# Order of layernorm parts and a third head on ScalarE in a fused two-layer transformer kernel

## The chip, the cores and the metric

The kernel runs on one core of a Trainium2 chip. A core has TensorE for matrix products, VectorE, ScalarE and GpSimd for elementwise work, and a SyncE that issues DMAs. Each works through its own queue, and they meet at semaphores. In the profile they are PE (PEld for its weight loads), DVE, ACT, POOL and SP. The metric is the device time of one execution in microseconds (us).

## The reference: what is computed

Two layers, each an attention and a feed-forward block, wrapped as `x = x + layernorm(block(layernorm(x)))`. The change lies in the second attention. It runs on 4 sequences (rows) of 1024 tokens with 256 features, in 16 heads of 16:

```python
scores = jnp.einsum('bhqd,bhkd->bhqk', q, k) / jnp.sqrt(jnp.asarray(HD, q.dtype))
w = jax.nn.relu(scores)
return w / (jnp.sum(w, axis=-1, keepdims=True) + KERN_EPS)
...
out = jnp.einsum('bhqk,bhkd->bhqd', attn, v)
out = out.transpose(0, 2, 1, 3).reshape(Bx, Sx, D)
out = out @ w_out + b_out
y = x + out
mu = jnp.mean(y, axis=-1, keepdims=True)
var = jnp.var(y, axis=-1, keepdims=True)
return (y - mu) * jax.lax.rsqrt(var + LN_EPS) * gamma + beta
```

The weights are a relu of the scores, divided by their sum; there is no exponential. The result is normalized once more and added to `x`, and the layernorm of that sum goes to the mixture-of-experts block that follows.

## The kernel before

**Stages.** The first layer ends at about 420 us, the second attention runs to about 1005 us, and the experts fill the rest. Only the second attention is touched.

**Tiling of the attention.** Loops run over rows (`b`, 4), blocks of 512 queries (`qh`, 2 per row), groups of four heads (`g`, 4) and tiles of 128 keys (`kt`, 8). The very last block is cut in two halves of 256 queries (`q2`, `halves = 2`), and a step then takes two key tiles. That makes 64 steps per row. One step is:

- `scores` (line 1489): 8 matmuls (16 in the last block), line 1501, for four heads. Two heads go to single PSUM banks (tag `s`, three buffers, also used by every other small product in the stage) and two to the halves of one two-bank tile `pair` (tag `d`, two buffers).
- The relu into `w`: ScalarE takes the two single heads (line 1510), VectorE the pair in one instruction over 1024 columns (line 1515). With `all_on_act` ScalarE takes the pair too (line 1513).
- `weigh` (line 1522), for scores of two steps earlier: the value matmuls of line 1527, which add into the one accumulator `po`. After the last key tile of a group, `finish` has VectorE transpose `po` into `turned` (line 1583), and the next group's first value matmuls must wait for that.

**Pieces and parts.** Everything else in the stage is cut into `Part` objects and worked in between. Those in `beside` are *pieces*, with matmuls of their own: transposes, keys, queries and values of the next row (`project`), the output projection (`project_out`, line 1292, evacuated by VectorE at line 1298), the transposes for the gate (`turn_gating`, line 1342) and the gate's logits (`gate`). Those in `rest` are called parts here: layernorm steps by tile of 128 tokens (statistics on VectorE, lines 1125 to 1127; the power on GpSimd, line 1128; centring, line 1303; `shift` on ScalarE, line 1315; the sum into `x` on VectorE, line 1320; the rows for the experts with their DMA stores, `token_rows`), the division by the weights' sum (`divide`, lines 1257 to 1267) and the fetching of keys.

**The planner.** The Python that writes the instructions keeps `late`, the work owed by VectorE, ScalarE and GpSimd in us. A step subtracts what the engine has to spare in it, a piece adds what it costs there and subtracts its time on TensorE, and a part is issued while the debt stays within `MOST` (0.8, 0.2, 0.4). A part can need others to have been called, some steps (`age`) before. In this stage the order on TensorE, VectorE and ScalarE is the order in which the Python issues.

**One step in the order of issue.** `scores` with its relus; then `go_on_with_oldest`, which calls `finish` and the piece (the piece first where `fresh` says that the last group's end had none); then `go_on`, which issues the parts that fit. So a part stands behind the piece's evacuation in the queues of VectorE and ScalarE.

**Which steps put all heads on ScalarE.** Steps with a piece of more than 1.5 us on TensorE; in the last row also one step per group.

Of the kernel before, what the change touches and what calls it, by code (L numbers as in the profile page):

```python
# [14 lines left out]
ALU = mybir.AluOpType  # L15
# [59 lines left out]
def kernel(  # L75
# [32 lines left out]
    nc = tc.nc  # L108
# [113 lines left out]
    with ExitStack() as st1:  # L222
# [96 lines left out]
        for r in range(2):  # L319
            for j in range(4):  # L320
                at = 32 * j + HD * r
# [29 lines left out]
        def open_row(hs=None, last=False):  # L351

            row = {"h": hs or [act4("h") for _ in range(BPB)], "last": last}
            row["q"], row["kT"] = {}, {}
            row["q_d"] = [[dram.tile([2 * P, 2, TB], F32, name="q_d") for _ in range(DC)] for _ in range(BPB)]
            row["k_d"] = [[dram.tile([2 * P, TB], F32, name="k_d") for _ in range(DC)] for _ in range(BPB)]

            row["v"] = act_v("vaug")
            return row
# [14 lines left out]
        def fetch_queries(row, k, t):  # L374

            q = row["q"][k, t] = acts.tile([P, 2, 2, TB], F32R, tag="gate", name="q")
            nc.gpsimd.dma_start(
                q.rearrange("p r s n -> p r (s n)"), row["q_d"][k][t].rearrange("(r p) s n -> p r (s n)", p=P)
            )
# [138 lines left out]
        class Chain:  # L518
# [11 lines left out]
            def finish(self):  # L530
                while self.steps:
                    self.go()
# [468 lines left out]
        def woven(left, own, to_hidden):  # L1001

            return [
                *left[:2], *own[:2], *left[2:], *own[2:-2],
                *to_hidden[:1], *own[-2:-1], *to_hidden[1:2], *own[-1:], *to_hidden[2:],
            ]  # L1010

        left, ffn, take = [], ([], [], []), {}
        for t in range(NB):
# [38 lines left out]
            beside = woven(left, own, to_hidden)  # L1052
# [49 lines left out]
    with ExitStack() as st3:  # L1102
# [74 lines left out]
        def in_order(parts):  # L1177

            return [parts[at] for at in sorted(parts, key=lambda at: (2.5 * at[0] + at[1], at))]

        def normalize(row, b, k):

            h, x = row["h"][k], xs[b * BPB + k]

            def stats(i):
                return scale_of("a", x[:, i, :])

            def apply(i, rs, ms):
                scaled(h[:, i, :], x[:, i, :], rs, ms)

            return by_tile((stats, 0, STATS), (apply, 2, {"pool": 0.6}))
# [294 lines left out]

            return [start]

        def scores(row, qh, q2, halves, g, kt, all_on_act):

            t, r = divmod(g, 2)
            n = TB // halves
            q0 = q2 * n
            w = wts.tile([P, 4, TB], F32, tag="w", name="w")
            singles = [ps.tile([P, TB], F32, tag="s", name="sc1", bufs=3) for _ in range(2)]
            pair = ps.tile([P, 2, TB], F32, tag="d", name="sc2", bufs=2)
            for m in range(halves):
                for part in (1, 0):
                    for j, sc in enumerate((*singles, pair[:, 0, :], pair[:, 1, :])):
                        rows = slice(32 * j, 32 * (j + 1))  # L1500
                        nc.tensor.matmul(  # L1501
                            sc[:, m * n : (m + 1) * n],
                            lhsT=row["kT"][t][rows, r, (kt + m) * P : (kt + m + 1) * P],
                            rhs=row["q"][qh, t][rows, r, part, q0 : q0 + n],
                            start=(part == 1),
                            stop=(part == 0),
                        )

            for j, sc in enumerate(singles):
                nc.scalar.activation(w[:, j, :], sc, AF.Relu)  # L1510
            if all_on_act:

                nc.scalar.activation(w[:, 2:4, :], pair, AF.Relu)  # L1513
            else:
                nc.vector.tensor_scalar(w[:, 2:4, :], pair, 0.0, None, ALU.max)  # L1515
            return w

        def weighed(halves, r):
# [19 lines left out]
        beside, rest = [], []  # L1538

        late, MOST = [0.0, 0.0, 0.0], (0.8, 0.2, 0.4)  # L1540

        def take(part):

            for i, us in enumerate(part.takes):
                late[i] += us - part.tensor
            part()

        def next_piece(keep=0):

            could = [part for part in beside if part.ready()]  # L1550
            return could[0] if len(could) > keep else None

        def do_piece(part):

            if part is not None:
                beside.remove(part)
                take(part)

        def go_on():

            k = 0
            while k < len(rest):
                part = rest[k]
                if part.ready() and all(us == 0.0 or l + us <= m for us, l, m in zip(part.takes, late, MOST)):
                    del rest[k]
                    take(part)
                    k = 0
                else:
                    k += 1
# [24 lines left out]
        row = row0  # L1594
        for k in range(BPB):
            add_bias(row, k)
        waiting, fresh = [], [False]

        def go_on_with_oldest(piece):

            at = waiting.pop(0)
            if fresh[0]:
                do_piece(piece)
            finish(*at)
            if ends(at):
                late[0] += 0.65 / at[4]
            if not fresh[0]:
                do_piece(piece)
            fresh[0] = ends(at) and (fresh[0] or piece is None)

        def ends(at):

            return at[6] == KT - at[4]

        def piece_for(at):

            soon_ends = at[4] == 1 and 1 < KT - at[6] <= 3
            return next_piece(1 if soon_ends and not fresh[0] else 0)

        for b in range(B):  # L1620
            after = open_row(None if b else next_hs, last=b + 2 == B) if b + 1 < B else None
            for qh in range(BPB):
                if (b, qh) == (B - 1, BPB - 1):

                    nc.scalar.activation(spare, row["h"][qh][:, 0, 0:1], AF.Exp)
                if after is not None:
                    ahead = normalize(after, b + 1, qh)
                    rest.extend(in_order(ahead))
                    rest.append(
                        Part(  # L1630
                            lambda to=(after, qh): beside.extend(project(*to)),
                            [(x, 1) for x in ahead.values()],
                        )
                    )
                halves = 2 if (b, qh) == (B - 1, BPB - 1) else 1
                for q2 in range(halves):
                    for g in range(NG):
                        for kt in range(0, KT, halves):
                            Part.now += 1
                            piece = piece_for(waiting[0]) if len(waiting) > 1 else None  # L1640
                            on_act = piece is not None and piece.tensor > 1.5
                            on_act = on_act or row["last"] and kt // halves % (8 // halves) == 4 // halves
                            w = scores(row, qh, q2, halves, g, kt, on_act)
                            waiting.append((row, b, qh, q2, halves, g, kt, w))
                            step = kt // halves
                            if step == 1 and g % 2 == 0:
                                if g == 0 and q2 == 0:
                                    fetch_queries(row, qh, 1)
                                elif g and halves == 1:
                                    fetch_queries(*((row, 1) if qh == 0 else (after, 0)), 0)  # L1650
                            for i, us in enumerate((1.62, -0.5, 1.62) if on_act else (0.4, 0.53, 1.62)):
                                late[i] -= us
                            if len(waiting) > 2:
                                go_on_with_oldest(piece)
                            go_on()
                            late[:] = [max(x, 0.0) for x in late]
            row = after
        while waiting:
            finish(*waiting.pop(0))
        while beside or rest:  # L1660
            Part.now += 1
            assert Part.now < 2000
            late[:] = [-2.0, -2.0, -2.0]
            do_piece(next_piece())
            go_on()
        state["close"][0](*divide(state, DC - 1))
    both.close()
# [4 lines left out]
    with ExitStack() as st4:  # L1672
# [260 lines left out]
        last = lists[NE - 1]  # L1933
# [294 lines left out]
```

## Time and profile before

| | us |
|---|---|
| median of 3 runs | 1529.57 |
| lowest, highest | 1524.9, 1531.48 |
| the profiled execution | 1527.67 |
| its span on the core | 1525.9 |

| 420 to 988 us of that span | TensorE | VectorE | ScalarE | GpSimd |
|---|---|---|---|---|
| busy, us of 568 | 550.4 | 419.0 | 383.7 | 172.4 |

| line | what | count | mean, ns |
|---|---|---|---|
| 1510 | ScalarE relu of one head, 512 columns | 512 | 595 |
| 1513 | ScalarE relu of two heads, 1024 columns | 63 | 1033 |
| 1515 | VectorE relu of two heads, 1024 columns | 193 | 1219 |
| 1583 | VectorE transpose of a group's result | 36 | 649 |
| 1298 | VectorE evacuation of an output projection, 512 columns | 15 | 692 |
| 1315 | ScalarE shift of a layernorm | 30 | 510 |

A row of the trace's groups and timelines reads: start and duration in us, engine, line, operation, what is written from what, count; in brackets the idle time just before it and what ended it. Two relus of ScalarE that run back to back are shown as one row of about 1.08 us. Busy time is an average over the stage; what a change is worth is read from the places where TensorE stands still. The ends of matmuls are modelled, so distances are taken from start to start.

### The profile page before, as it was taken

The page shows a single profiled execution, that of the slowest core. Times are in us where ns is not written, and L with a number is a line of the kernel's source. Part 1 is how long each engine was busy: PE and PEld are TensorE (multiplying, and loading weights), DVE is VectorE, ACT ScalarE, POOL GpSimd, SP SyncE. Part 2 cuts the span into 40 slices and gives each one's busy share as a digit, 9 for nine tenths or more (in the row PEclk, how much of TensorE's full clock was granted, in tenths as well). Part 3 has the DMA queues.
Part 4 walks back from the last instruction along what each step waited for, and adds up shares of the span by engine and source line. Part 5 has one row for each costly group of instructions (what it writes and reads, how often), then busy time and mean ns, then how long its engine had stood idle before and what let it go on. Part 6 is the DMA issues. An engine that isn't in the chain of part 4 may idle for free. (4 is left out here: it accounts for less than half of the span.)

```text
span 1525.9 us, 24163 instructions
## 1 busy us (share of the span) xinstructions
PE 1462.9 (96%) x9286; PEld 787.0 (52%) x9286; DVE 887.4 (58%) x2128; ACT 685.0 (45%) x1160; POOL 495.7 (32%) x627
## 2 busy tenths in 40 slices
PE   8999999999899999999999999849999999999996
PEld 4666666667532323332333325427566656665674
DVE  5456654656457598759775887675545631212145
ACT  4244455443466666766666677622221122112142
POOL 4123232222341223422432223303425233242554
PEclk9999999999999999999999999979999999999998
DMA  8400000003423331542244211151314234233264
GB/s 217 131 1 1 1 1 1 1 0 117 120 83 125 94 108 49 166 120 87 64 147 138 70 50 36 43 156 38 100 28 116 49 73 94 53 78 77 65 162 128
DMA packets 91885, 121.58 MB, mean 80 GB/s; under 512 B 24925, under 2 KB 64250, under 8 KB 91642
## 3 DMA queue, kind: packets, MB, share of 16 engines
q1 hardware_dynamic: 70000, 73.09, 15.5%
q0 software_dynamic: 21712, 46.94, 13.3%
q8 instruction: 73, 1.20, 0.3%
q14 instruction: 42, 0.34, 0.1%
q10 hardware_dynamic: 58, 0.01, 0.0%
HBM read 66.90 MB, written 53.12 MB: 79 GB/s over the span
## 5 line engine op out<-in xcount | busy, mean ns | idle before, releaser
L1510 ACT ACTIVATE w<-sc 128x512 f32<-128x512 f32 x512 | 278.0, 595 | 141.9 <-ACT w L1510 60.4
L1527 PE MATMUL po<-w,vaug 128*17 128x512 f32 (+1 forms) x2304 | 270.1, 552 | 11.6 <-DVE turned L1583 11.3
L1515 DVE TENSOR_SCALAR w<-sc 128x1024 f32<-128x1024 f32 x193 | 234.4, 1219 | 43.2 <-PE sc L1501 37.1
L2110 ACT ACTIVATE hid<-ph,mb 128x512 f32<-128x512 f32 (+1 forms) x136 | 89.9, 662 | 340.5 <-PE ph L2103 244.7
L2103 PE MATMUL ph<-xT,w 128*128 128x512 f32 (+1 forms) x544 | 229.7, 574 | 0.3 <-DVE xT L2086 0.3
L2120 PE MATMUL py<-w,hid 128*128 128x256 f32 x1024 | 229.7, 380 | 0.0
L2120 PEld LDWEIGHTS py<-w,hid 128*128 128x128 f32 x1024 | 191.7, 190 | 31.7 <-issue 6.7
L1501 PE MATMUL sc<-q,kT 32*128 32x512 f32 (+1 forms) x2304 | 195.2, 413 | 6.9 <-DVE w L1515 4.8
L1501 PEld LDWEIGHTS sc<-q,kT 32*128 32x128 f32 x2304 | 88.4, 184 | 182.4 <-ACT w L1510 122.6
L2141 POOL DMA_INDIRECT acc_d<-y,idx x56 | 88.6, 1582 | 226.1 <-DVE y L2140 101.3
L2103 PEld LDWEIGHTS ph<-xT,w 128*128 128x128 f32 x544 | 99.7, 190 | 107.6 <-issue 98.4
L2139 DVE TENSOR_TENSOR y<-py,mb 128x256 f32<-128x256 f32 x56 | 23.5, 420 | 126.7 <-PE py L2120 116.0
L1527 PEld LDWEIGHTS po<-w,vaug 128*17 128x17 f32 x2304 | 41.8, 95 | 104.8 <-issue 74.2
L1911 POOL DMA_INDIRECT got<-tok_d,idx x64 | 66.5, 1039 | 62.4 <-DVE counts L1745 24.5
L1513 ACT ACTIVATE w<-sc 128x1024 f32<-128x1024 f32 x63 | 65.1, 1033 | 0.0
L2086 DVE COPY xT<-tp 128x512 f32<-128x512 f32 (+1 forms) x34 | 22.2, 659 | 71.7 <-PE tp L2081 63.9
L724 PE MATMUL pg<-nT,wh 128*128 128x512 f32 x128 | 61.6, 613 | 1.5 <-ACT nT L663 1.5
L850 PE MATMUL py<-wo,oT 128*128 128x256 f32 x256 | 61.9, 385 | 0.0
L740 PE MATMUL pv<-wh,nT 128*128 128x512 f32 x128 | 59.7, 592 | 0.0
L850 PEld LDWEIGHTS py<-wo,oT 128*128 128x128 f32 x256 | 47.2, 190 | 17.1 <-issue 9.6
L915 ACT ACTIVATE hid<-ph,vec 128x512 f32<-128x512 f32 x64 | 39.8, 685 | 27.3 <-PE ph L906 27.1
L588 POOL TENSOR_TENSOR x<-x,y 128x1024 f32<-128x1024 f32 x13 | 30.6, 2354 | 57.4 <-ACT y L577 57.4
(307 smaller groups left out, 2035.3 us busy)
## 6 DMA issues: line engine op xcount, KB each, us to landing
q<-q_d POOLq DMA_DIRECT2D x16, 1024.0 KB
w<-in_L_ffn_W_dram SPq DMA_DIRECT2D x16, 1024.0 KB
q_d<-parts SPq DMA_DIRECT2D x48, 256.0 KB
kT<-k_d POOLq DMA_DIRECT2D x16, 512.0 KB
k_d<-parts SPq DMA_DIRECT2D x24, 256.0 KB
acc_d<-logits SPq DMA_DIRECT2D x8, 512.0 KB
tok_d<-hg SPq DMA_DIRECT2D x32, 128.0 KB
x<-in_L_attn_x_dram SPq DMA_DIRECT2D x7, 512.0 KB
```

The lines of the kernel that those rows point to most:

```text
L724: nc.tensor.matmul(pg, lhsT=wh[:, c, HID + e * P : HID + (e + 1) * P], rhs=d["nT"][:, c, :], start=(c == 0), stop=(c == DC - 1),)
L850: nc.tensor.matmul(py, lhsT=d["oT"][:, e, :], rhs=wo[:, e, :], start=(e == 0), stop=(e == EC - 1))
L1501: nc.tensor.matmul(sc[:, m * n : (m + 1) * n], lhsT=row["kT"][t][rows, r, (kt + m) * P : (kt + m + 1) * P], rhs=row["q"][qh, t][rows, r, p ...
L1510: nc.scalar.activation(w[:, j, :], sc, AF.Relu)
L1513: nc.scalar.activation(w[:, 2:4, :], pair, AF.Relu)
L1515: nc.vector.tensor_scalar(w[:, 2:4, :], pair, 0.0, None, ALU.max)
L1527: nc.tensor.matmul(po[32 * j : 32 * j + HD + 1, weighed(halves, r)], lhsT=row["v"][:, kt + m, HQ * t + 4 * r + j, :], rhs=w[:, j, m * n : ...
L1911: return nc.gpsimd.indirect_dma_start(out=dst, out_offset=None, in_=rows[:, :], in_offset=self.at_chunk(c), bounds_check=NT - 1, oob_is_er ...
L2103: nc.tensor.matmul(ph, lhsT=w1[:, c, f * P : (f + 1) * P], rhs=xT[u][:, c, h * n : (h + 1) * n], start=(c == 0), stop=(c == DC - 1),)
L2110: nc.scalar.activation(hid[:, f, h * n : (h + 1) * n], ph, AF.Gelu, bias=mb1[:, e * FC + f : e * FC + f + 1])
L2120: nc.tensor.matmul(py, lhsT=hid[:, f, i * P : (i + 1) * P], rhs=w2[:, f, :], start=(f == 0), stop=(f == FC - 1),)
L2141: scatter = nc.gpsimd.indirect_dma_start(out=acc_d[:, :], out_offset=lists[e].at_chunk(k), in_=y, in_offset=None, bounds_check=NT - 1, oob ...
```

## The change

Three things change, all in the planner of the second attention.

1. `scores` gets a number of heads for ScalarE: 2, 3 or 4. With 3, ScalarE takes the first half of `pair` in an instruction of its own, and VectorE's relu covers only the other half, 512 columns.
2. `heads_on_act` chooses. Four with a piece of more than 1.5 us on TensorE. Otherwise two, if ScalarE owes time or a part with ScalarE work is ready. Otherwise three, if the step has the end of a group and no piece, or if it is the last row and parts are left; else two. The last row's one step per group with four heads is gone. `HEADS` holds what each choice leaves the engines to spare.
3. `take` only books a piece, and the piece is called later. In `go_on_with_oldest` the piece is booked first, then `finish` (unless `fresh`), then `go_on` issues the parts, and only then the piece is called. With `fresh` the parts come first, then the piece, then `finish`. A part that needs the piece itself is therefore not ready before the next step.

```diff
-            for j, sc in enumerate(singles):
+            for j, sc in enumerate((*singles, pair[:, 0, :])[: 2 if on_act == 4 else on_act]):
                 nc.scalar.activation(w[:, j, :], sc, AF.Relu)
-            if all_on_act:
-
+            if on_act == 4:
                 nc.scalar.activation(w[:, 2:4, :], pair, AF.Relu)
             else:
-                nc.vector.tensor_scalar(w[:, 2:4, :], pair, 0.0, None, ALU.max)
+                j = on_act - 2
+                nc.vector.tensor_scalar(w[:, 2 + j : 4, :], pair[:, j:2, :], 0.0, None, ALU.max)
             return w
...
             for i, us in enumerate(part.takes):
                 late[i] += us - part.tensor
-            part()
...
-        def do_piece(part):
-
-            if part is not None:
-                beside.remove(part)
-                take(part)
...
                     del rest[k]
                     take(part)
+                    part()
                     k = 0
...
             at = waiting.pop(0)
+            if piece is not None:
+                beside.remove(piece)
+                take(piece)
             if fresh[0]:
-                do_piece(piece)
-            finish(*at)
-            if ends(at):
-                late[0] += 0.65 / at[4]
-            if not fresh[0]:
-                do_piece(piece)
+                go_on()
+                if piece is not None:
+                    piece()
+                finish(*at)
+            else:
+                finish(*at)
+                if ends(at):
+                    late[0] += 0.65 / at[4]
+                go_on()
+                if piece is not None:
+                    piece()
             fresh[0] = ends(at) and (fresh[0] or piece is None)
...
+        def heads_on_act(piece, at_end, last):
+
+            if piece is not None and piece.tensor > 1.5:
+                return 4
+            if late[1] > 0.0 or any(part.ready() and part.takes[1] for part in rest):
+                return 2
+            return 3 if piece is None and at_end or last and len(rest) > 0 else 2
+
+        HEADS = {2: (0.4, 0.53, 1.62), 3: (0.96, 0.04, 1.62), 4: (1.62, -0.5, 1.62)}
...
-                            on_act = piece is not None and piece.tensor > 1.5
-                            on_act = on_act or row["last"] and kt // halves % (8 // halves) == 4 // halves
+                            on_act = heads_on_act(piece, len(waiting) > 1 and ends(waiting[0]), row["last"])
                             w = scores(row, qh, q2, halves, g, kt, on_act)
...
-                            for i, us in enumerate((1.62, -0.5, 1.62) if on_act else (0.4, 0.53, 1.62)):
+                            for i, us in enumerate(HEADS[on_act]):
                                 late[i] -= us
                             if len(waiting) > 2:
                                 go_on_with_oldest(piece)
-                            go_on()
+                            else:
+                                go_on()
...
-            do_piece(next_piece())
+            piece = next_piece()
+            if piece is not None:
+                beside.remove(piece)
+                piece()
             go_on()
```

More of the change, by code (lines that the diff above doesn't have):

```diff
@@ L1487, in close, with scores @@
             return [start]
-        def scores(row, qh, q2, halves, g, kt, all_on_act):
+        def scores(row, qh, q2, halves, g, kt, on_act):
             t, r = divmod(g, 2)
```

## The prediction

> **What bounds the kernel now.** I read the page first (TensorE busy 96% of the span), then found the stage that the edit touches: its score matmuls (line 1501) run from 420.1 to 984.9 us. In that stretch TensorE is busy nearly throughout, so time can only be won where it stands still. The view of waits, limited to TensorE and 420 to 988 us, names what it waits for; its columns are total, times, longest:
>
> ```profile
> PE po L1527 <- DVE turned L1583: 11.3, 15, 2.9
> PE sc L1501 <- DVE w L1515: 4.8, 6, 1.2
> ```
>
> Both end on VectorE: one when the transpose of a finished group is late and the single accumulator `po` can't be reused, the other when VectorE's relu of two heads is late and the `pair` bank isn't free. Ends of matmuls are modelled, so I took lost time from starts instead. In the timeline of TensorE an undisturbed step is 0.67 us from the first score matmul to the first value matmul and 0.98 us on to the next run: 1.65 us. The excess over that at each disturbed step, added up:
>
> - ends of groups, rows 0 to 2: .49, .73, .85, .67, .15, .85, .67, .15, .85 = 5.4 us;
> - the second step after an output projection, rows 0 to 2: 1.25 (540.97 and 543.60), 1.66 (590.75), 1.35, 1.67, 1.35 = 7.3 us;
> - row 3: ends of 512-column groups .67, .78, .61, .49, .84 = 3.4; a step after a projection (872.29) 1.3; ends of 256-column groups .98, .45, .37, .23 = 2.0; the place at 962.79 with the steps behind it 2.98 + .49 + .85 + .11 = 4.4; together 11.1 us.
>
> That is 23.8 us, the most that this edit can win in the stage. The cause of the second kind is seen in VectorE's own timeline around 590 us:
>
> ```profile
> 587.56 0.69 DVE L1298 TENSOR_TENSOR y<-pt,h 128x512 f32<-128x512 f32 x1 [2.53 <-PE pt L1288]
> 588.16 0.42 DVE L1125 BATCH_NORM_STATS2 sta<-x 128x6 f32<-128x256 f32 x1
> ...
> 591.05 0.15 DVE L1127 TENSOR_SCALAR veb<-mvb 128x1 f32<-128x1 f32 x1
> 591.14 1.23 DVE L1515 TENSOR_SCALAR w<-sc 128x1024 f32<-128x1024 f32 x1
> ```
>
> VectorE stood idle 2.53 us for the projection, evacuated it, and only then worked off four layernorm statistics (588.16 to 591.14); the relu of scores issued at 587.45 started at 591.14. Three of the four read `x` and could have run in the idle time. The largest place is the same story; first VectorE, then TensorE:
>
> ```profile
> 961.23 0.69 DVE L1298 TENSOR_TENSOR y<-pt,h 128x512 f32<-128x512 f32 x1 [2.90 <-PE pt L1288]
> 961.84 0.42 DVE L1125 BATCH_NORM_STATS2 stg<-x 128x6 f32<-128x256 f32 x1
> ...
> 964.80 1.22 DVE L1515 TENSOR_SCALAR w<-sc 128x1024 f32<-128x1024 f32 x1
> 965.94 0.44 DVE L1583 STREAM_TRANSPOSE turned<-po 128x256 f32<-128x256 f32 x1
> ```
>
> ```profile
> 962.79 0.74 PE L1501 MATMUL sc<-q,kT 32*128 32x256 f32 x16
> 966.44 1.11 PE L1527 MATMUL po<-w,vaug 128*17 128x256 f32 x16 [2.91 <-DVE turned L1583]
> 967.48 1.23 PE L1501 MATMUL sc<-q,kT 32*128 32x256 f32 x16
> ```
>
> **What the Trainium skill says.** PSUM — Partial Sum Buffer, Engine vs sequencer instructions: the queues of ScalarE and VectorE are strict FIFO. The trace agrees: 2.53 us idle with ready statistics behind. TensorE: Matmul & The Clock Gate, What's actually happening: the clock falls after an idle window of about 3.4 us. Here the clock averaged 0.83 over 965 to 975 us, after the hole of 3 us, and the next steps took 1.16 and 1.84 us for .67 and .99. The same PSUM page, PSUM bank collisions: two engines must not read one bank at once. The third head is its own bank of `pair` (512 fp32), so ScalarE and VectorE may read beside each other; no run here shows it.
>
> **The change by parts.** *(a) Three heads on ScalarE.* VectorE's relu of 1024 columns (1.22 us) becomes one of 512. That form isn't in the trace; the nearest row is `y<-pt,h`, 512 columns from PSUM, 0.69 us. So VectorE gains 0.53 us per such step. ScalarE's two heads take 1.08 us together, 0.595 alone, hence 0.49 for each further one: 1.57 us for three. From above, three times 0.595 is 1.79; from ScalarE: Activation LUTs, What ACT_TABLE_LOAD costs (186 ns + 0.833 per column, overlap 93) my estimate is 3 x 612 - 2 x 93 = 1.65. I take 1.57, against a step of 1.65; ScalarE just keeps up, and the function falls back to two heads whenever it owes time.
>
> At a group's end, VectorE's order is relu(n), transpose. At 475.25 the relu ran 474.50 to 475.73, the transpose 475.64 to 476.35, `po` went on at 476.41, 0.49 late. With a relu of 0.69 the transpose waits for the last value matmul only. The floor is .15, seen where a transposition piece follows (575.70). So in rows 0 to 2: .34 + .53 + .52 + .52, and for the three ends of .85, where layernorm parts crowd and a ready shift forbids three heads, half of .53 each, .8: **2.7 us**. The two of .15 stay.
>
> In row 3 three heads apply at any step without a large piece while layernorm parts are left. They replace the old rule, all four on ScalarE once per group (12 of 64 steps). Ends of 512-column groups: .52 + .53 + .46 + .34 + .53 = 2.4. Of 256 columns, where the transpose takes 0.44 and the floor is nothing: .53 + .45 + .37 + .23 = 1.6. Together **4.0 us**.
>
> *(b) Layernorm parts before the evacuation.* No instruction is added or removed; VectorE (and ScalarE's shift, 0.51) run what is ready while the piece's matmuls run. VectorE waited 46.4 us for `parts` of keys, 22.4 of queries and 16.9 for `y` in this stage: that is the room. Each instruction hides under 1.9 us of piece, and the planner's budget (0.8 us owed, measured 0.75 for statistics priced 0.72) holds better, as it never counted the wait. At 590.75 the three `sta` (2.2 us) move into the 2.53 us of idling and the relu follows the evacuation at 588.25. I count 85% of the 7.3 us in rows 0 to 2, **6.2**, and of 872.29, **1.1**; the rest because the statistics of the piece's own output, now not ready until the piece is called, come a step later with up to 0.8 us owed. At 962.79 three `stg` move into 2.90 us of idling; the relu then ends near 963.2, the transpose at 963.65, against 963.46 when `po` would be wanted. No hole, so the clock doesn't fall either: 90% of 4.4, **4.0**.
>
> What is issued with the parts moves too: `token_rows` stores on SyncE now stand ahead of the piece's `q_d` or `k_d` stores, two per tile and one of `x_d`. The fetch of keys is held six steps back, over 10 us, which hides it; GpSimd already waits 75.2 us for `k_d` off the path. If that cover went, its pow and scaling of rows would come late, and behind them the shift on ScalarE and then its relus. GpSimd's own order isn't changed. The evacuation is what is late next: its bank is wanted by the second step after, 1.65 us after the piece's end; with the 0.69 of the evacuation that leaves some 0.85 us of slack, and an owed 0.8 fits.
>
> *Against it.* The last half tile's chain has no slack: its layernorm ends with transposes at 987.86, directly at the end of `po`; one step later for its statistics costs 1.65, **1.7**. New stalls from a changed plan the trace can't show: between nothing and all of the gain; I take **3**.
>
> Sum: 2.7 + 4.0 + 6.2 + 1.1 + 4.0 - 1.7 - 3 = 13.3 us. The profiled execution took 1527.67 us (span 1525.9 and 1.8 around it), so it becomes 1514.4 (span 1512.6); it lay 1.9 under the median of 1529.57, so the forecast is **1516 us**, its own range 1508 to 1522.
>
> **The rivals.** *ScalarE becomes the bound of row 3.* For: 1.57 of 1.65 leaves nothing. Against: the fallback to two heads. At 1.79 it loses 0.135 us on some 45 steps, 6 us: 1522.
> *The debt only moves.* Statistics put a step later meet the next relu there, and the 6.2 + 1.1 of (b) and half of (a) are given back: 11 less, 1527. Three heads hardly ever chosen in rows 0 to 2 would be part of this. Against: VectorE was busy 419 of 568 us, so room exists.
> *Slower: the piece's bank.* Layernorm parts ahead hold up the evacuation, the piece's bank (one of three) isn't free, and TensorE stops after each piece. 39 pieces have an evacuation on VectorE (15 `y`, 24 `parts`). It begins where parts overrun by more than 0.85 us, and decides (slower by over 0.5%) from a mean stop of (13.3 + 7.65) / 39 = 0.54 us; at 0.7 it costs 27: 1543. For: parts may wait for GpSimd's pow or ScalarE's shift inside the queue, which no budget counts. Against: the same parts stood before the next relu already, and TensorE bore it.
> *Even better:* every hole closes and the last chain ends earlier: 24 us, 1505.
>
> **Numbers.** Forecast 0.68, better 0.04, ScalarE's bound 0.08 (a quarter of it still faster), debt 0.09, bank 0.11. About 0.5% (7.6 us) is what can be told from no change: faster 0.68 + 0.04 + 0.02 = 0.74, same 0.06 + 0.09 = 0.15, slower 0.11. The range 1507 to 1533 leaves out the slower case and about half of the best.
>
> **What would show it.** Right: the hole at 590 us and its likes in rows 1 and 2 gone, statistics before `y<-pt,h`, TensorE's waits for `turned` and `w` from 16 to under 5 us, relu rows of 512 at about 0.69, no fall of the clock near 960, the stage ending about 13 us sooner. Wrong: TensorE waiting for a ScalarE relu in row 3, waits of score matmuls for `y<-pt,h` or `parts`, or a longer stretch after the last value matmul.

## The result and the profile after

The changed kernel is slower: 1535.76 us (median of 14 runs, 1533.56 to 1538.7) against 1529.9 us (14 runs). The ratio is 1.004, with a 95% interval of 1.003 to 1.0051. The forecast was 1516 us, a gain of 0.9%.

The profiled execution took 1538.66 us, its span 1536.9: 11.0 us more than the one before. It is one of the five slower of the 14 runs, which took 1537.9 to 1538.7 us at a mean granted clock of 0.982 to 0.984, where the other nine took 1533.6 to 1536.3 at 0.986 to 0.988. The waits of TensorE in the same stage (total, times, longest, in us), in the changed kernel:

```profile
PE po L1527 <- DVE turned L1577: 24.2, 22, 1.5
PE sc L1501 <- ACT w L1510: 0.9, 3, 0.5
```

Score matmuls no longer wait for VectorE's relu, which had been 4.8 us. Value matmuls wait twice as long as before (11.3 us) for the transpose of a finished group. What VectorE waits for, in the changed kernel:

```profile
DVE w L1515 <- ACT w L1510: 43.7, 42, 2.0
DVE w L1515 <- PE sc L1501: 31.8, 45, 3.0
```

The first line has no counterpart before: VectorE's relu now stands still for ScalarE's relu, 42 times. The end of the third group shows it. Before (VectorE, then ScalarE, then TensorE; start and duration in us):

```profile
474.50 1.23 DVE L1515 TENSOR_SCALAR w<-sc 128x1024 f32<-128x1024 f32 x1 [0.43 <-PE sc L1501]
475.64 0.71 DVE L1583 STREAM_TRANSPOSE turned<-po 128x512 f32<-128x512 f32 x1
```

```profile
474.42 1.08 ACT L1510 ACTIVATE w<-sc 128x512 f32<-128x512 f32 x2 [0.57 <-ACT w L1510]
```

```profile
475.25 0.74 PE L1501 MATMUL sc<-q,kT 32*128 32x512 f32 x8
476.41 1.05 PE L1527 MATMUL po<-w,vaug 128*17 128x512 f32 x8 [0.42 <-DVE turned L1583]
```

The same place in the changed kernel (the row of five relus joins the three of this step and the two of the next):

```profile
476.36 1.23 DVE L1515 TENSOR_SCALAR w<-sc 128x1024 f32<-128x1024 f32 x1 [0.42 <-PE sc L1501]
479.54 0.69 DVE L1515 TENSOR_SCALAR w<-sc 128x512 f32<-128x512 f32 x1 [1.95 <-ACT w L1510]
480.15 0.71 DVE L1577 STREAM_TRANSPOSE turned<-po 128x512 f32<-128x512 f32 x1
```

```profile
477.93 2.73 ACT L1510 ACTIVATE w<-sc 128x512 f32<-128x512 f32 x5 [0.57 <-ACT w L1510]
```

```profile
477.78 1.05 PE L1527 MATMUL po<-w,vaug 128*17 128x512 f32 x8
478.76 0.74 PE L1501 MATMUL sc<-q,kT 32*128 32x512 f32 x8
480.91 1.05 PE L1527 MATMUL po<-w,vaug 128*17 128x512 f32 x8 [1.41 <-DVE turned L1577]
```

The relu of 512 columns takes 0.69 us, as forecast. It could have started at about 478.0, when the step's scores were there, as the relu before it did. It starts at 479.54, as ScalarE's third relu ends (477.93 and three heads). The transpose is behind it on VectorE, and the next group's value matmuls come 1.48 us late, where they had come 0.49 us late.

The other half of the change, the order of parts, did what was said of it. VectorE in the changed kernel, at the output projection that had left a hole of 1.66 us:

```profile
591.35 0.68 DVE L1298 TENSOR_TENSOR y<-pt,h 128x512 f32<-128x512 f32 x1
591.95 0.42 DVE L1125 BATCH_NORM_STATS2 sta<-x 128x6 f32<-128x256 f32 x1
...
594.73 0.69 DVE L1298 TENSOR_TENSOR y<-pt,h 128x512 f32<-128x512 f32 x1
595.54 1.23 DVE L1515 TENSOR_SCALAR w<-sc 128x1024 f32<-128x1024 f32 x1
```

Between the two evacuations VectorE works on statistics and centring, with no gap above 0.1 us. The scores of 594.62 have their relu at 595.54.

Lost time on TensorE, counted from start to start as in the prediction (its hand sums differ by a few tenths), tells where the time went. The last column is not lost time but the stretch from the end of the last value matmul to the experts' first count. The runs e1 to e7 are described below. All numbers are us, of the profiled executions:

| kernel | first steps | ends, rows 0-2 | other, rows 0-2 | ends, row 3 | other, row 3 | sum | stretch after |
|---|---|---|---|---|---|---|---|
| before | 1.5 | 5.2 | 7.5 | 7.3 | 3.8 | 25.3 | 19.6 |
| changed | 4.3 | 14.4 | 0.5 | 12.4 | 1.9 | 33.5 | 22.0 |
| e1 VectorE first | 1.5 | 2.8 | 0.5 | 0.8 | 1.4 | 7.0 | 20.1 |
| e2 order of parts | 2.8 | 5.6 | 0.5 | 8.7 | 0.7 | 18.3 | 20.7 |
| e3 heads, old order | 4.2 | 13.1 | 7.6 | 10.4 | 3.2 | 38.5 | 19.6 |
| e4 heads, old order, VectorE first | 1.5 | 2.0 | 7.6 | 5.5 | 5.3 | 21.9 | 19.6 |
| e5 two tiles | 4.2 | 3.6 | 0.5 | 0.8 | 0.5 | 9.6 | 20.6 |
| e6 group ends only | 1.5 | 2.8 | 0.5 | 5.0 | 0.7 | 10.5 | 20.7 |
| e7 third head first | 1.5 | 5.7 | 0.5 | 3.6 | 10.5 | 21.8 | 20.8 |

The changed kernel loses 9.2 + 5.1 us more at the ends of groups and gains 7.0 + 1.9 elsewhere. The first steps of the stage (+2.8) are a matter of the execution: the granted clock was 0.84 between 414 and 436 us in this one and 1.00 in the one before. Of the runs below, e3 and e5 show 0.84 there, e2 0.92 and the others 1.00, and the loss goes with it: 4.2 or 4.3 us, 2.8 and 1.5. e1 has the same instructions in this stretch as the changed kernel. That, and a profiled run before that lay 2.2 us under its median, is why the two profiles lie 11.0 us apart and the medians 5.9.

### The profile page after: what moved, and what is told of

Its sections match the earlier page's. It is cut to its first block, busy times and chain, and to the rows that moved or that the text cites. A ratio compares the mean times of both kernels' runs of the same rounds, so it can differ in the third digit from the quotient of the medians.

```text
span 1536.9 us, 24162 instructions
## 1 busy us (share of the span) xinstructions
PE 1465.8 (95%) x9286; PEld 787.5 (51%) x9286; DVE 875.4 (57%) x2140; ACT 701.4 (46%) x1201; POOL 495.9 (32%) x627
## 5 line engine op out<-in xcount | busy, mean ns | idle before, releaser
L1510 ACT ACTIVATE w<-sc 128x512 f32<-128x512 f32 x565 | 303.8, 596 | 135.1 <-issue 44.4
L1515 DVE TENSOR_SCALAR w<-sc 128x1024 f32<-128x1024 f32 (+1 forms) x205 | 221.2, 1083 | 77.1 <-ACT w L1510 43.7
L850 PEld LDWEIGHTS py<-wo,oT 128*128 128x128 f32 x256 | 47.3, 190 | 17.1 <-issue 9.6
L1512 ACT ACTIVATE w<-sc 128x1024 f32<-128x1024 f32 x51 | 52.7, 1032 | 0.0
```

The source lines that it names most:

```text
L850: nc.tensor.matmul(py, lhsT=d["oT"][:, e, :], rhs=wo[:, e, :], start=(e == 0), stop=(e == EC - 1))
L1515: nc.vector.tensor_scalar(w[:, 2 + j : 4, :], pair[:, j:2, :], 0.0, None, ALU.max)
```

## The experiments

Three theories were put against each other. *Wait*: VectorE's relu is made to wait for ScalarE's third head, and the transpose is behind it. *ScalarE*: three heads are too much for ScalarE. *Order*: the new order of parts costs the time. The ratios of e1 to e4 are to 1528.34 us for the kernel before (14 runs), those of e5 to e7 to 1529.48 (27 runs), each measured beside them.

**e1, VectorE first.** One line moves; plan and instructions stay.

```diff
-            for j, sc in enumerate((*singles, pair[:, 0, :])[: 2 if on_act == 4 else on_act]):
+            for j, sc in enumerate(singles):
                 nc.scalar.activation(w[:, j, :], sc, AF.Relu)
...
                 nc.vector.tensor_scalar(w[:, 2 + j : 4, :], pair[:, j:2, :], 0.0, None, ALU.max)
+                if j:
+                    nc.scalar.activation(w[:, 2, :], pair[:, 0, :], AF.Relu)
```

> The changed kernel with one thing moved: in a step with three heads VectorE's relu of its half of the pair is issued ahead of ScalarE's relu of the other half; plan and instructions are the same. Theory 'wait' (the relu of VectorE is made to wait for ScalarE's third head, and the transpose of the group stands behind it): that wait of 43.7 us is gone, the waits of value matmuls for the transpose fall from 24.2 us to under 9, and the time falls by 13 to 18 us, to about 1519. Theory 'ScalarE' (three heads are simply too much for ScalarE in a step of 1.65 us): nothing changes, about 1535. Theory 'order' (the later plan and the longer tail cost the time): 1532 to 1535.

Measured: 1511.26 us, ratio 0.9892 (0.9875 to 0.9909). That is 17.1 us under the kernel before, and so some 23 under the changed kernel, where 13 to 18 were expected. The waits for the transpose fall to 2.6 us. The same group's end, VectorE and then ScalarE:

```profile
474.90 0.69 DVE L1515 TENSOR_SCALAR w<-sc 128x512 f32<-128x512 f32 x1 [0.42 <-PE sc L1501]
475.79 0.72 DVE L1579 STREAM_TRANSPOSE turned<-po 128x512 f32<-128x512 f32 x1 [0.20 <-PE po L1529]
```

```profile
474.81 1.08 ACT L1510 ACTIVATE w<-sc 128x512 f32<-128x512 f32 x2 [0.56 <-ACT w L1510]
475.78 0.61 ACT L1517 ACTIVATE w<-sc 128x512 f32<-128x512 f32 x1
```

VectorE starts with the scores, is done at 475.59, and waits 0.20 us for the value matmuls. ScalarE's third head now stands behind VectorE's relu in the program, and the wait has changed sides:

```profile
ACT w L1517 <- DVE w L1515: 2.4, 6, 0.7
```

It costs nothing at this place, since ScalarE gets to its third head only after its two single heads, at 475.78. "Wait" holds; "ScalarE" and "order" fall, as the heads and the plan are the same. This version beats both kernels.

**e2, the order of parts.** The changed kernel with its plan, but VectorE keeps both heads of the pair where the plan says three.

```diff
-            for j, sc in enumerate((*singles, pair[:, 0, :])[: 2 if on_act == 4 else on_act]):
+            for j, sc in enumerate(singles):
...
-                j = on_act - 2
-                nc.vector.tensor_scalar(w[:, 2 + j : 4, :], pair[:, j:2, :], 0.0, None, ALU.max)
+                nc.vector.tensor_scalar(w[:, 2:4, :], pair, 0.0, None, ALU.max)
```

> The changed kernel with its whole plan and order, but where the plan says three heads ScalarE takes two and VectorE the pair of 1024 columns as before. Theory 'wait': no VectorE relu waits for ScalarE, the ends of groups cost .5 to .85 us again instead of 1.48, the holes after projections stay closed; rows 0 to 2 about 10 us shorter than in the changed kernel; in row 3 the plan overrates VectorE by 0.53 us in some 40 steps, so stops come back there; 1522 to 1530. Theory 'order': no better than 1533.

Measured: 1522.58 us, ratio 0.9955 (0.9938 to 0.9971). The holes after projections stay closed (0.5 us in rows 0 to 2, from 7.5), and the ends of groups are as before (5.6). The order of parts is a gain by itself. In row 3 the ends cost 8.7. That fits a plan that counts on a relief which this kernel doesn't give, but the four-head step per group is gone too, and no run tells the two apart.

**e3 and e4, three heads in the old order.** The kernel before with its own plan, and three heads where the new rule asks for it: e3 issues ScalarE's third head first, e4 VectorE's relu. The bookkeeping stays that of before. Shown is the line that chooses; the edit of `scores` is that of the change in e3 and that of e1 in e4.

```diff
-                            w = scores(row, qh, q2, halves, g, kt, on_act)
+                            heads = 4 if on_act else heads_on_act(piece, len(waiting) > 1 and ends(waiting[0]), row["last"])
+                            w = scores(row, qh, q2, halves, g, kt, heads)
```

> The kernel before with its whole plan and order (the four-head steps too), but with three heads on ScalarE, third head ahead of VectorE's relu, where the new rule asks for it. Theory 'wait': the ends of groups without a piece go from .5 to .85 us to about 1.5 and those of the last block from .4 to 1.1, holes after projections stay: 8 to 14 us slower than before, 1538 to 1544. Theory 'ScalarE': the same here. Theory 'order': as before, 1525 to 1531.

> As the run with three heads in the old plan and order, but VectorE's relu is issued ahead of ScalarE's third head. Theory 'wait': the ends of groups fall to about .15, 5 to 8 us faster than before, 1522 to 1525. Theory 'ScalarE': as slow as its twin, 1538 or more. Theory 'order': 1525 to 1531.

Measured: e3 1538.19 us, ratio 1.0068 (1.0054 to 1.0083); e4 1524.19 us, ratio 0.9971 (0.996 to 0.9981). Both times lie where "wait" put them; but the undisturbed ends in e4 cost 0.24 us, not 0.15. In e3 the wait is back in the old order. VectorE's waits there:

```profile
DVE w L1515 <- ACT w L1510: 38.4, 33, 2.3
```

The same three heads lose 0.7% with the one order of issue and win 0.3% with the other. Alone, the order of parts wins 0.45% and e4's heads 0.3%; together, in e1, 1.1%. The surplus is in row 3: its ends and other places cost 11.1 us before, 9.4 in e2, 10.8 in e4 and 2.2 in e1. There the new plan and the third head gain only together.

**e5, two tiles.** The changed kernel, third head of ScalarE issued first as it was, but the pair is two tiles of one bank each. Relus of two heads become two instructions.

```diff
-            pair = ps.tile([P, 2, TB], F32, tag="d", name="sc2", bufs=2)
+            pair = [ps.tile([P, TB], F32, tag=f"d{i}", name=f"sc{2 + i}", bufs=2) for i in range(2)]
...
+            for j, sc in enumerate((*singles, *pair)):
+                if j < on_act:
+                    nc.scalar.activation(w[:, j, :], sc, AF.Relu)
+                else:
+                    nc.vector.tensor_scalar(w[:, j, :], sc, 0.0, None, ALU.max)
```

> The changed kernel, plan and order as they are (ScalarE's third head still issued first), but the two banks of the pair are two tiles of their own, so each engine reads a tile that the other doesn't. VectorE's relu of two heads becomes two instructions of 512 columns, about 0.1 us more per such step, and ScalarE's of the pair likewise. Theory 'shared tile' (the wait exists only because both engines read one tile): no VectorE relu waits for ScalarE, ends of groups about .24 us as in the run with VectorE first, 1512 to 1518. Theory 'issue order or banks' (it takes VectorE first, or the chip itself keeps them apart): as the changed kernel, 1533 or more.

Measured: 1512.53 us, ratio 0.9883 (0.9863 to 0.9903). The same group's end, ScalarE and then VectorE:

```profile
477.80 1.58 ACT L1511 ACTIVATE w<-sc 128x512 f32<-128x512 f32 x3 [0.56 <-ACT w L1511]
477.91 0.69 DVE L1513 TENSOR_SCALAR w<-sc 128x512 f32<-128x512 f32 x1 [0.39 <-issue]
```

VectorE's relu runs within ScalarE's three, here beside the two single heads. At another step it runs beside the third (878.73 to 879.34), which reads the other half of what had been the pair:

```profile
877.76 1.58 ACT L1511 ACTIVATE w<-sc 128x512 f32<-128x512 f32 x3 [0.17 <-ACT x L1315]
878.55 0.68 DVE L1513 TENSOR_SCALAR w<-sc 128x512 f32<-128x512 f32 x1
```

So the two engines can read the two banks at once; the wait was in the program because both instructions read one tile, although not the same half of it. That they write one tile, `w`, isn't the reason: they do so here and before as well. The traces don't tell where the banks lie, so nothing is shown for two banks that are neighbours.

**e6, three heads at group ends only.** As e1, with the plan unchanged, but two heads at the other steps of row 3 where the plan says three.

```diff
+                            ending = piece is None and len(waiting) > 1 and ends(waiting[0])
-                            w = scores(row, qh, q2, halves, g, kt, on_act)
+                            w = scores(row, qh, q2, halves, g, kt, 2 if on_act == 3 and not ending else on_act)
```

> The run with VectorE first, plan unchanged, but three heads only at the ends of groups without a piece; at the other steps of the last row where the plan says three, VectorE keeps both heads of the pair. If the gain of the third head lies in the ends of groups alone, about 1512 to 1514; if the last row needs the relief in all its steps, the debts come back there, 0.53 us in each of some 30 steps: 1515 to 1521.

Measured: 1515.01 us, ratio 0.9915 (0.9898 to 0.9932), 3.8 us over e1 by the medians and 3.5 by the ratios. The time lies on the lower edge of the second expectation. Row 3 loses 5.7 us instead of 2.2, all of the difference at ends. So the relief in the other steps of row 3 is worth some 3 us, much less than 0.53 us in each of some 30 steps.

**e7, the third head first on ScalarE.** The changed kernel; ScalarE does its half of the pair before the two single heads, which shortens VectorE's wait without removing it.

```diff
+            if on_act == 3:
+                nc.scalar.activation(w[:, 2, :], pair[:, 0, :], AF.Relu)
-            for j, sc in enumerate((*singles, pair[:, 0, :])[: 2 if on_act == 4 else on_act]):
+            for j, sc in enumerate(singles):
```

> The changed kernel with ScalarE doing its head of the pair first and the two single heads after it, so that VectorE's wait is one head long instead of three. Theory 'wait': VectorE's relu starts about 1 us sooner, ends of groups cost about .5 us instead of 1.48 (the waits for the transpose near 10 us in place of 24), 1516 to 1521. Theory 'ScalarE' or 'order': as the changed kernel, 1533 or more.

Measured: 1526.6 us, ratio 0.998 (0.9971 to 0.9989). At most ends of groups the expectation holds: 0.52 us in place of 1.48. VectorE waits for one head (the profile itself counts only 0.7 us of waits for the transpose, where about 10 was expected: the row of scores before it is stretched to 1.07 us, so that little of the stop shows as idle time):

```profile
475.69 0.69 DVE L1517 TENSOR_SCALAR w<-sc 128x512 f32<-128x512 f32 x1 [1.00 <-ACT w L1510]
476.29 0.71 DVE L1579 STREAM_TRANSPOSE turned<-po 128x512 f32<-128x512 f32 x1
```

The time as a whole misses the expectation by 5.6 us and lies between the two expectations. The single heads are evacuated half a microsecond later, and one of their banks is what the next step's scores need. A step in row 3 (ScalarE, then TensorE):

```profile
863.60 1.08 ACT L1512 ACTIVATE w<-sc 128x512 f32<-128x512 f32 x2
863.92 1.06 PE L1501 MATMUL sc<-q,kT 32*128 32x512 f32 x8
```

The first score matmul starts at 863.92, the next only at 864.24, just after ScalarE's first single head ends (864.19); the row takes 1.06 us in place of 0.74. Nearly every step with three heads in row 3 stops 0.32 to 0.38 us in this way, 10.5 us in all other places of row 3 where e1 has 1.4. A shorter wait was traded for a new one.

## Why the prediction was wrong

The step that failed is in part (a): the relu of one head was taken to start when its scores are there, so that "the transpose waits for the last value matmul only". It started when ScalarE's third head was done, 1.5 us later. I had asked whether the chip lets both engines read the pair, and it does (e5); I had not asked whether the program lets them, with both reading one tile. The change makes them share it for the first time: before, each tile of scores was read by one engine. No rival had this wait. One rival, the piece's bank, had the sign right, but by another cause: it looked for stops after pieces, and in rows 0 to 2 the changed kernel loses 14.4 us at ends of groups and 0.5 in all other places. e1 alone tells against all of the rivals: ScalarE's load, the moved debt and the piece's bank are the same there, and it is 1.1% faster than before.

Point by point, with e1 as the change free of that wait:

- *Third head, 0.69 us on VectorE, 1.57 on three heads of ScalarE:* measured 0.69 and 1.58. ScalarE keeps up, as said.
- *Ends of groups in rows 0 to 2, a gain of 2.7:* 5.2 to 2.8, so 2.4. The floor at an end without a piece is 0.24, not the 0.15 taken from an end with one. In the changed kernel this term was a loss of 9.2.
- *Parts before the evacuation, 6.2 in rows 0 to 2:* 7.5 to 0.5, so 7.0, in the changed kernel too. The mechanism and its size were right.
- *Row 3, 4.0 + 1.1 + 4.0 = 9.1:* 11.1 to 2.2, so 8.9. In the changed kernel a loss of 3.2. The hole at 962.79 is gone in both. One of the stops was misread: the 0.84 listed as the end of a 512-column group (918.92) is a wait for ScalarE's relu (0.46 us in the profile), which stood behind an ACT_TABLE_LOAD of 1.28 us on ScalarE at 916.21. A shorter relu on VectorE was no remedy for it, and 0.66 of it is left in e1.
- *The last chain one step late, 1.7:* the stretch after the last value matmul grew by 0.5 in e1 and 1.1 in e2. In the changed kernel by 2.4: there, as in e2, the transposes for the gate wait 1.09 us for the last half tile's layernorm, and then the granted clock was 0.57 over 1001 to 1004, where e2 had 1.00 at the same matmuls.
- *Stalls in new places, 3:* none of that size in rows 0 to 2 (0.5 in all). An allowance against an unknown plan, it was not needed.

With the wait gone the sum of 13.3 compares with 2.4 + 7.0 + 8.9 - 0.5 = 17.8 us, which is what lies between the two spans (1525.9 and 1508.1); between the medians it is 17.1. So the forecast was a little cautious for the change as it was meant. As it was written, three heads turned a gain of 11 us at the ends and in row 3 into a loss of 12.

## What to carry to other kernels

When a change gives one tile to two engines, ask which waits the program will hold, not only whether the hardware allows it. Here the two readers of one tile were kept in their order of issue, whichever came first (e1 and the changed kernel), although they read different halves. Issue first the instruction that others wait behind, or give each engine a tile of its own. And look at what queues behind the instruction that waits: here 0.69 us of work carried a transpose with it on which TensorE depended.

## What the runs showed of the hardware that was not expected

Two things are worth keeping. ScalarE and VectorE read two banks at the same time without slowing each other: 1.58 us for three relus and 0.69 for one while they overlap (e5), and the same 1.58 and 0.69 where VectorE waits (the changed kernel). The clock granted to TensorE differed where the work was the same: 0.84 and 1.00 over the first 22 us of the stage, which made 2.8 us of difference in the profiles without any edit behind it, and 0.57 and 1.00 after the same wait of 1.09 us at the end of the stage (the changed kernel and e2). A single profile isn't to be read closer than that.
